# Fetching some chunks of a two-layer graph convolution row by row through SyncE

## The chip, the cores and the metric

The kernel runs on one core of one Trainium2 chip. The metric is the device time of one execution in microseconds. The kernel before the change takes 2024.17 us in the median of three runs (2023.47 to 2024.36).

## The reference

The input is a table of 6250 nodes with 512 features in float32 and a list of 100000 edges, sorted by their target node. Two Chebyshev graph convolutions follow each other, and the input is added at the end:

```
edge_index = jnp.stack([src, dst])
norm = -dinv[src] * dinv[dst]                  # dinv = 1/sqrt(out-degree), 0 for degree 0
def cheb_conv(x, W0, W1, b):
    tx1 = segment_sum(x[src] * norm[:, None], dst, num_segments=6250)
    return x @ W0 + tx1 @ W1 + b
h = relu(layernorm(x))
h = cheb_conv(h, W1_0, W1_1, b1)
h = layernorm(h) * gamma + beta
h = where(h >= 0, h, 0.01 * h)
out = x + cheb_conv(h, W2_0, W2_1, b2)
```

The part that matters here is `x[src]`: for every edge the row of its source node (512 float32, 2 KB) is fetched from a table in HBM, 100000 rows in each layer, and the rows of one target node are summed.

## The kernel before

The sorted edges are cut into 782 chunks of 128 edges. One chunk is one gather: `gather_to` lets GpSimd (POOL in the profile) issue one indirect DMA at L480, which reads 128 source indices from a column of `sidx` (for the last 270 chunks of layer 1 from `lidx`) and brings 128 rows, one into each partition, from the table of the layer, `tab[layer]`. A row of `tab[0]` is 528 floats wide: 512 features, then a scale of the row in column 512. The rows land in `places`, a tile of 63 places of 528 floats per partition, used as a ring: `slot(k)` names the place of the chunk with the running number k, and `zr(layer, t)` is the view of its 512 features. Of the 63 places the last 8 are lent to the second layer's weights (`w_late`, W2_1 and W2_0, loaded half way through layer 0), which leaves a ring of R = 55. The first 75 chunks of layer 0 are gathered straight from the input (L250) and put through layer norm on the chip; 27 chunks of layer 1 are gathered early, at L490 (`gather_ahead`).

Three chunks make a unit, and four units, so 12 chunks, a group; a layer has 66 groups. The loop over the groups g does, in this order: issue gathers as far as R chunks ahead of what has been summed; finish the node blocks that are complete (`finished`, `turn`); build the selection matrices `sel` on VectorE (`choose`; in layer 0 `scale`, L647, multiplies them by the rows' own scale out of column 512); sum the group on TensorE (`sums`, L660: one matmul of 128x32 by 128x512 for each chunk, into a PSUM tile `ps`); copy to `agg` (L673). A node block has 128 nodes, so there are 49 blocks a layer. For each block the sums are placed (`place`, L693), transposed (L803) and multiplied by the weights (`products`, L568), and `finish` writes the block: in layer 0 to `tab[1]` (L777) and `h_tab` (L782), in layer 1 to the output (L757).

The orders of TensorE, GpSimd and SyncE (SP) are written out by hand: what the loop emits first is issued first. SP's queue holds only ordinary DMAs: in layer 0 for each block the load of the block's own rows (`load_h`, L545), L777 and L782; in layer 1 L545, the load of the input's rows (L564) and L757. Several of them wait for TensorE or VectorE, and those behind them wait too.

Of the kernel before, what the change touches and what calls it, by code (L numbers as in the profile page):

```python
# [9 lines left out]
F32 = mybir.dt.float32  # L10
BF = mybir.dt.bfloat16
I32 = mybir.dt.int32
AF = mybir.ActivationFunctionType
OP = mybir.AluOpType
AX = mybir.AxisListType
# [3 lines left out]
SP = mybir.EngineType.SP  # L19

P = 128
# [4 lines left out]
Q = 32  # L26
NQ = P // Q
STEP = 3
DRIFT = 32
RE = 14  # L30
RAW = 76
PAD = 16
LATE = 3
AHEAD_OF = 27
JOIN = 12


def parts(r):
# [5 lines left out]
def gnn_kernel(  # L44
# [33 lines left out]
    nc = tc.nc  # L78
    N, D = x.shape
# [6 lines left out]
    NC = -(-E // P)  # L86
# [3 lines left out]
    NS = -(-NU // NQ)  # L90
    unit = [max(0, NU - NQ * (NS - g)) for g in range(NS + 1)]
    rows = [min(P, N - i * P) for i in range(NB)]
    LAST = 18
    W = D + PAD

    const = ctx.enter_context(tc.tile_pool(name="const", bufs=1))
# [6 lines left out]
    tab = [dram.tile([n, w], F32, name=f"tab{i}") for i, (n, w) in enumerate(((NB * P, W), (N + 1, D)))]  # L103
    zero_row = (NB - LATE) * P
# [3 lines left out]
    ident = const.tile([P, P], F32, name="ident")  # L108
    iota_r = const.tile([P, P], F32, name="iota_r")
    ones = const.tile([P, 1], F32, name="ones")  # L110
    eps = const.tile([P, 1], F32, name="eps")
# [16 lines left out]
    e_src = const.tile([P, AHEAD_OF, LATE], F32, name="e_src")  # L128
    w_sb = [const.tile([P, KD, D], F32, name=f"w{i}") for i in range(2)]
    sc = const.tile([P, 2, NB], F32, name="sc")  # L130
    pick = const.tile([P, P], BF, name="pick")
    src_lo = const.tile([P, P], BF, name="src_lo")
    src_hi = const.tile([P, RAW], F32, name="src_hi")
    p_id = const.tile([P, 1], F32, name="p_id")

# [288 lines left out]
    n_unseen = usual_path(tc, locals())  # L424
    stay.close()
    with tc.If(n_unseen > 0):
        general_path(tc, x, src, dst, bias1, bias2, gam, bet, w_sb, (W2_1, W2_0), dinv, ndinv, ident, iota_r,
                     eps, out)


def usual_path(tc, have):
    nc = tc.nc
    (x, out, tab, h_tab, ndinv, sidx, dlx, iota_r, w_sb, W2_1, W2_0, w_late, ident, eps, ones, first, nodes_ps, node_of, minus,
     unsorted, dinv, sdinv, bias1, bias2, gam, bet, unseen, unit, N, E, D, NB, NC, NU, NS, KD, rows, places, R,
     load_rest, sc, pick, src_lo, src_hi, eidx, e_src, zero_row, p_id, lent, X) = (
        have[n] for n in ("x out tab h_tab ndinv sidx dlx iota_r w_sb W2_1 W2_0 w_late ident eps ones first nodes_ps node_of "
                          "minus unsorted dinv sdinv bias1 bias2 gam bet unseen unit N E D NB NC NU NS KD rows places "
                          "R load_rest sc pick src_lo src_hi eidx e_src zero_row p_id lent X").split())
    AHEAD = 2
    SOON = range(3, 6)  # L440
    EARLY = {NB - 4: NS - 13, NB - 3: NS - 11, NB - 2: NS - 9, NB - 1: NS - 7}
# [9 lines left out]
    with ExitStack() as es:  # L451
# [11 lines left out]

        LATER = places.shape[1] - R

        def slot(k):
            return k - X if k < X + R + LATER else (k - X - LATER) % R

        def zr(layer, t):
            k = layer * NC + t  # L470
            return lent[k] if k < X else places[:, slot(k), :D]

        def gather_to(layer, summed_to):
            nonlocal gathered
            end = summed_to + R
            if layer == 0:
                end = max(end, min(end + LATER, X + LATER + 2 * R))
            for t in range(gathered, min(end, NC)):
                own_scale = layer == 0 and t >= RAW
                nc.gpsimd.indirect_dma_start(  # L480
                    out=places[:, slot(t), :] if own_scale else zr(layer, t), out_offset=None,
                    in_=x if layer == 0 and t < RAW else tab[layer],
                    in_offset=bass.IndirectOffsetOnAxis(
                        ap=lidx[:, t - SHIFTED : t - SHIFTED + 1] if layer and t >= SHIFTED else sidx[:, t : t + 1], axis=0))
            gathered = max(gathered, min(end, NC))
# [149 lines left out]
        def scale(sel, chunk, of=(0, NQ)):  # L635

            at = chunk[0][0]
            start = max(chunk[of[0]][0], RAW)
            end = chunk[min(of[1], len(chunk)) - 1][-1] + 1
            if end <= start:  # L640
                return
            each = sel.rearrange("p q s e -> p (q s) e")
            cut = sorted({start, end} | {t for t in range(start + 1, end) if slot(t) != slot(t - 1) + 1})
            for lo, hi in zip(cut, cut[1:]):
                v = each[:, lo - at : hi - at, :]
                k = slot(lo)
                last = nc.vector.tensor_tensor(  # L647
                    v, v, places[:, k : k + hi - lo, D : D + 1].to_broadcast([P, hi - lo, Q]), op=OP.mult)
            return last

        def sums(layer, g, sel, chunk, cnt=None, some=None, opens=True, closes=True):

            n = len(chunk)
            if opens:
                summed[0] = psum.tile([P, D], F32, name="ps")
            ps = summed[0]
            if some is None:
                some = [(s, q) for s in range(STEP) for q in range(n) if s < len(chunk[q])]
            for s, q in some:
                nc.tensor.matmul(ps[q * Q : (q + 1) * Q, :], sel[:, q, s, :], zr(layer, chunk[q][s]), start=(s == 0),  # L660
                                 stop=(s == len(chunk[q]) - 1 and (cnt is None or chunk[q][0] >= AHEAD_OF)))
            for b in range(LATE if cnt is not None else 0):
                r = rows[NB - LATE + b]
                for q in range(n):
                    if chunk[q][0] < AHEAD_OF:
                        nc.tensor.matmul(ps[q * Q : (q + 1) * Q, :], cnt[:r, b, q * Q : (q + 1) * Q],
                                         late[NB - LATE + b][:r], start=False, stop=(b == LATE - 1))
            if closes:
                wide = layer == 0 and g < SOON.stop + 2 and g % 2
                agg[g] = pool.tile([P, D], F32, name="pre" if wide else "agg", bufs=3)  # L670
                w = D // 2 if g == NS - 1 else D
                for lo in range(0, D, w):
                    nc.scalar.activation(agg[g][: n * Q, lo : lo + w], ps[: n * Q, lo : lo + w], AF.Copy)  # L673
# [212 lines left out]
        for layer in range(2):  # L886
# [5 lines left out]
            for g in range(NS - 1):  # L892
                gather_to(layer, STEP * unit[g])
                if layer == 0 and g == NS // 2:
                    for k, w in enumerate((W2_1, W2_0)):
                        nc.sync.dma_start(w_late[:, k], w.rearrange("(k p) d -> p k d", p=P))
                if layer == 0:
                    look_up("hT_ps")
                    find("hT_ps")
                    assert looked >= min(RAW, STEP * unit[g + 1])  # L900
                due = []

                def finished():
# [14 lines left out]
                if g == NS - 2 and layer == 0:  # L918
                    assert i >= NB - LATE and gathered == NC
                    gather_ahead()  # L920
                sel, chunk = chosen.pop(g) if g in chosen else choose(g)
                if layer == 0:
                    with ExitStack() as order:
                        for ins in behind.values():
                            order.enter_context(tc.issue_after(ins.ins))
                        scaled = scale(sel, chunk)
# [10 lines left out]
                if g < NS - 2:  # L937
                    sums(layer, g, sel, chunk, cnt)
                    if soon:
                        i, left = finished()  # L940
                else:
                    assert len(due) == 1 and due[0][0] == NB - 3 and all(len(c) == STEP for c in chunk)
                    if layer:
                        half = [[(s, q) for s in range(STEP) for q in range(at, at + NQ // 2)] for at in (0, NQ // 2)]
                        step = [half[0][:-2], half[0][-2:], half[1]]
                    else:
                        step = [[(s, q) for q in range(NQ)] for s in range(STEP)]
                    sums(layer, g, sel, chunk, None, step[0], True, False)
                    k, (hT, an) = due.pop()
                    aT = first_half(layer, k, hT, an, lambda: sums(layer, g, sel, chunk, None, step[1], False, False))  # L950
                    second(layer, k, aT)
                    sums(layer, g, sel, chunk, None, step[2], False, True)
                if layer == 0 and g == 12:
                    own_row[0] = pool.tile([P, D], F32, name="xt")
                    nc.vector.tensor_scalar_mul(own_row[0][:, : rows[END]], ident[:, : rows[END]], ndinv[:, END : END + 1])
# [70 lines left out]
    return n_unseen  # L1026


def general_path(tc, x, src, dst, bias1, bias2, gam, bet, w_sb, w_late, dinv, ndinv, ident, iota_r, eps,
                 out):  # L1030


# [31 lines left out]
    z_tab = [dram.tile([N, D], F32, name=f"z_tab{i}") for i in range(2)]  # L1064
    e_src = dram.tile([NC, P], I32, name="e_src")
    e_dst = dram.tile([NC, P], I32, name="e_dst")
    w_sb = list(w_sb)
    for k, w in enumerate(w_late):
        w_sb.append(const.tile([P, KD, D], F32, name=f"w_late{k}"))
# [284 lines left out]
```

## Time and profile before

| What | Value |
|---|---|
| median of the three runs | 2024.17 us |
| profiled execution | 2021.09 us, of which the span from the first to the last instruction is 2019.3 us |
| TensorE busy | 1669.7 us (83%), 6907 matmuls |
| GpSimd busy | 1488.9 us (74%), 1578 instructions |
| VectorE busy | 707.6 us (35%) |
| ScalarE busy | 414.3 us (21%) |
| moved by DMA | 528.41 MB, 262 GB/s |
| mean granted TensorE clock | 0.917 |

The busy time of GpSimd counts only the part of an indirect DMA in which its descriptors are made; the time between two of them counts as idle. The issue of a DMA by SP isn't counted as busy time of an engine at all; the views of a single line show it. The DMA share is the mean busy share of the core's 16 DMA engines.

### The profile page before, as it was taken

Reading aid. Unit: us, or ns where it says so; the run is one execution under the profiler, and the core shown is the slowest. Engines: PE = TensorE matmul, PEld = TensorE weight load, DVE = VectorE, ACT = ScalarE, POOL = GpSimd, SP = SyncE. Lnnn points to the kernel's source line nnn. Section 1 sums busy time; section 2 is a strip of 40 time slices with the busy share of each in tenths; the row PEclk is TensorE's granted clock in tenths of the full one; section 3 lists DMA queues with packets and bytes.
Section 4 is the critical chain, followed back from the end, with each engine's and each line's share of the span. In section 5 each row is a group of like instructions: output and inputs, shape, how many; then the busy total and the mean of one; then the engine's idle time right before and its main releaser. Section 6 shows DMA issues by size and latency. Waiting matters only on the chain.

```text
span 2019.3 us, 20097 instructions
## 1 busy us (share of the span) xinstructions
PE 1669.7 (83%) x6907; PEld 669.5 (33%) x6907; DVE 707.6 (35%) x1498; ACT 414.3 (21%) x752; POOL 1488.9 (74%) x1578
## 2 busy tenths in 40 slices
PE   5579998776887776888879888888888888888988
PEld 4444443222333222333323322323332223333333
DVE  7975554333354334343363111112221212222211
ACT  7895221111121111121111010011010001011100
POOL 6477777777777777777777777777777777777774
PEclk8789999888998888989999998889999989989999
DMA  9998888888988888888887787788787878788875
GB/s 329 396 374 269 267 269 263 249 258 245 303 265 253 251 260 241 267 266 260 245 261 241 245 257 247 247 252 255 240 255 246 254 244 257 241 263 251 272 235 171
DMA packets 190131, 528.41 MB, mean 262 GB/s; under 512 B 34652, under 2 KB 36426, under 8 KB 190020
## 3 DMA queue, kind: packets, MB, share of 16 engines
q0 software_dynamic: 125120, 415.88, 67.7%
q1 hardware_dynamic: 64860, 111.14, 15.2%
q8 instruction: 56, 0.92, 0.2%
q14 instruction: 55, 0.45, 0.1%
q10 hardware_dynamic: 40, 0.02, 0.0%
HBM read 475.25 MB, written 51.66 MB: 261 GB/s over the span
## 4 chain that ended last, share of the span: by engine, by line
PE 39%; DMA 31%; POOL 12%; issue 10%; DVE 5%; ACT 2%; POOLq 0%; DVEq 0%; SPq 0%; ACTq 0%
DMA places<-tab,sidx 24%; PE u_ps L568 16%; POOL places L480 12%; PE ps L660 12%; PE an_ps L693 7%; DMA places<-tab,lidx 5%; PE hT_ps L556 1%; PE hT_ps L803 1%; DVE hi L362 1%; DVE lo L362 1%; ACT places L539 1%; DMA dst_c<-in_dst_dram 1%; DMA tab<-places 1%; PE both_ps L379 1%; DVE sel L647 0%
## 5 line engine op out<-in xcount | busy, mean ns | idle before, releaser
L480 POOL DMA_INDIRECT places<-tab,sidx x1191 | 1130.5, 949 | 363.4 <-issue 256.2
L660 PE MATMUL ps<-places,sel 128*32 128x512 f32 x3104 | 517.1, 671 | 145.4 <-DMA places<-tab,sidx 81.9
L693 PE MATMUL an_ps<-agg,there 128*128 128x512 f32 (+1 forms) x554 | 270.0, 620 | 88.2 <-ACT agg L673 83.2
L480 POOL DMA_INDIRECT places<-tab,lidx x270 | 255.3, 946 | 82.3 <-issue 60.9
L660 PEld LDWEIGHTS ps<-places,sel 128*32 128x32 f32 x3104 | 103.1, 117 | 524.1 <-issue 190.0
L607 DVE TENSOR_TENSOR sel<-dlx,nodes_ps 128x384 f32<-128x384 f32 (+3 forms) x134 | 72.4, 541 | 415.1 <-PE ps L660 415.1
L568 PE MATMUL u_ps<-w,hT 128*128 128x512 f32 (+1 forms) x400 | 185.3, 607 | 20.6 <-ACT hT L558 20.1
L673 ACT ACTIVATE agg<-ps 128x512 f32<-128x512 f32 (+2 forms) x130 | 76.1, 587 | 570.1 <-PE ps L660 545.1
L568 PE MATMUL u_ps<-places,hT 128*128 128x512 f32 (+2 forms) x408 | 182.4, 591 | 2.9 <-ACT hT L558 2.9
L568 PE MATMUL u_ps<-w,aT 128*128 128x512 f32 x384 | 173.2, 594 | 2.7 <-DVE aT L805 2.7
L693 PEld LDWEIGHTS an_ps<-agg,there 128*128 128x128 f32 (+1 forms) x554 | 105.8, 199 | 209.6 <-issue 109.8
L568 PE MATMUL u_ps<-places,aT 128*128 128x512 f32 x384 | 173.5, 594 | 0.8 <-DVE aT L805 0.8
L647 DVE TENSOR_TENSOR sel<-sel,places 128x384 f32<-128x384 f32 (+11 forms) x71 | 34.4, 490 | 328.3 <-DMA places<-tab,sidx 323.2
L754 DVE TENSOR_TENSOR u_ps<-u_ps,bias 128x512 f32<-128x512 f32 x45 | 31.5, 700 | 281.8 <-PE u_ps L568 281.8
L558 ACT ACTIVATE hT<-hT_ps 128x512 f32<-128x512 f32 (+1 forms) x98 | 58.2, 594 | 278.1 <-PE hT_ps L556 277.6
L796 ACT ACTIVATE an<-an_ps,ndinv 128x512 f32<-128x512 f32 x96 | 65.8, 685 | 213.7 <-PE an_ps L693 213.5
L681 DVE TENSOR_SCALAR there<-iota_r,node_of 128x128 f32<-128x128 f32 (+1 forms) x286 | 85.8, 302 | 63.6 <-PE an_ps L693 61.3
L568 PEld LDWEIGHTS u_ps<-w,hT 128*128 128x128 f32 (+1 forms) x400 | 73.7, 195 | 96.5 <-issue 74.7
L766 ACT ACTIVATE sd<-mv,eps 128x1 f32<-128x1 f32 (+1 forms) x49 | 14.4, 294 | 433.5 <-DVE mv L764 433.5
L250 POOL DMA_INDIRECT places<-in_x_dram,sidx x63 | 60.0, 952 | 54.0 <-ACT junk L266 21.1
L568 PEld LDWEIGHTS u_ps<-places,hT 128*128 128x128 f32 (+1 forms) x408 | 74.4, 192 | 76.5 <-issue 71.5
L568 PEld LDWEIGHTS u_ps<-w,aT 128*128 128x128 f32 x384 | 70.7, 190 | 83.0 <-issue 77.8
(197 smaller groups left out, 1318.6 us busy)
## 6 DMA issues: line engine op xcount, KB each, us to landing
places<-tab,sidx POOLq DMA_INDIRECT x1191, 3.8
h_tab<-g SPq DMA_DIRECT2D x48, 256.0 KB
xt<-in_x_dram SPq DMA_DIRECT2D x48, 256.0 KB
out_dram<-t SPq DMA_DIRECT2D x48, 256.0 KB
tab<-t SPq DMA_DIRECT2D x46, 256.0 KB
tab<-places SPq DMA_DIRECT2D x22, 528.0 KB
h<-tab SPq DMA_DIRECT2D x45, 256.0 KB
h<-h_tab SPq DMA_DIRECT2D x45, 256.0 KB
```

What stands on the lines that cost most here:

```text
L250: nc.gpsimd.indirect_dma_start(out=lent[t] if t < X else places[:, t - X, :D], out_offset=None, in_=x, in_offset=bass.IndirectOffsetOnAxis ...
L362: nc.vector.tensor_tensor(t, s[:, g * 2 * GJ : (g + 1) * 2 * GJ].rearrange("p (j s) -> p j s", s=2)[:, :, None, :] .to_broadcast([EP, GJ, ...
L480: nc.gpsimd.indirect_dma_start(out=places[:, slot(t), :] if own_scale else zr(layer, t), out_offset=None, in_=x if layer == 0 and t < RAW ...
L558: nc.scalar.activation(hT[:, :, :r], ps[:, :, :r], AF.Copy)
L568: nc.tensor.matmul(u_ps[:r], hT[:, kc, :r], w[:, kc, :], start=(start and kc == 0), stop=(stop and kc == KD - 1))
L607: nc.vector.tensor_tensor(sel[:, q : q + k, :w, :], of, node[:, q : q + k, None, :].to_broadcast([P, k, w, Q]), op=OP.is_equal)
L647: last = nc.vector.tensor_tensor(v, v, places[:, k : k + hi - lo, D : D + 1].to_broadcast([P, hi - lo, Q]), op=OP.mult)
L660: nc.tensor.matmul(ps[q * Q : (q + 1) * Q, :], sel[:, q, s, :], zr(layer, chunk[q][s]), start=(s == 0), stop=(s == len(chunk[q]) - 1 and ( ...
L673: nc.scalar.activation(agg[g][: n * Q, lo : lo + w], ps[: n * Q, lo : lo + w], AF.Copy)
L681: behind[1] = nc.vector.tensor_scalar(t[:m, :r], iota_r[:m, :r], node_of[:m, g : g + 1], -(1.0 + i * P), op0=OP.subtract, op1=OP.is_equal)
L693: nc.tensor.matmul(placed[i][:r], t[:m, :r], agg[g][:m, :], start=(g == inside[i][0]), stop=(g == inside[i][-1]))
L796: nc.scalar.activation(an[:r], placed.pop(i)[:r], AF.Copy, scale=ndinv[:r, i : i + 1])
```

## The change

Fifteen chunks are no longer gathered by GpSimd: 7 of layer 0 (t = 206, 290, ..., 710) and 8 of layer 1 (t = 146, 230, ..., 734). Each is the last chunk of its group. SP fetches their 128 rows with 128 DMAs of one row each. For that SP loads the byte offsets of up to 9 rows from SBUF into registers (`starts`, made by `set_starts` from `src` with one DMA and a few VectorE operations for each layer) and issues one DMA per row with that register in its source address. A row is cut into 16 pieces: of 33 floats in layer 0 (the last of the 16 pieces ends with the scale; the pieces overlap by one float in the source, and the place is 16 x 33 floats), of 32 floats in layer 1. `fetch` is called twice in every group, once ahead of `finished` and once after the sums, and issues up to 9 rows each time, so 18 rows a group; it begins at group 7 of layer 0 and group 2 of layer 1. Two whole groups lie between the group that issues a chunk's last row and the group that sums the chunk.

In layer 0 the rows go to two of the places that W2_1 holds later, and the load of W2_1 moves from the middle of layer 0 to four groups before its end. In layer 1 they go to the tile of W1_0, which layer 1 no longer reads; `general_path`, which runs only for inputs that the usual path does not cover, therefore loads W1_1 and W1_0 again. `gather_to` skips the 15 chunks, `zr` gives the view of 16 pieces for them, the matmul's target is seen in the same shape, and `scale` multiplies such a chunk in an operation of its own.

```diff
+AT_ONCE = 9
+PIECES = (16, 16)
+ONE_BY_ONE = (7, 2)
+SECOND = 32
...
+    low_of = const.tile([P, 2, P], BF, name="low_of")
+    pick, src_lo = (low_of[:, k, :] for k in range(2))
+    starts = low_of.rearrange("p k e -> p (k e)").bitcast(I32)
...
+        one_by_one, to_fetch = {}, []
+        for layer, g in enumerate(ONE_BY_ONE):
+            for j in range(SECOND):
+                at = g + -(-P * (j + 1) // (2 * AT_ONCE)) + 2
+                if at > NS - 5:
+                    break
+                t = STEP * unit[at + 1] - 1
+                one_by_one[layer * NC + t] = (layer * SECOND + j, R + j % 2 if layer == 0 else j % 2)
...
+        def set_starts():
...
+                nc.sync.dma_start(starts[rows_of], bass.AP(tensor=src.tensor, offset=src.offset + some[0] * P,
+                                                           ap=[[step * P, n], [1, P]]))
+                nc.vector.tensor_copy(at, starts[rows_of])
+                if layer:
+                    nc.vector.tensor_single_scalar(up, at, float(zero_row), op=OP.is_ge)
+                    nc.vector.tensor_add(at, at, up)
+                nc.vector.tensor_scalar_mul(at, at, 4.0 * tab[layer].shape[1])
+                nc.vector.tensor_copy(starts[rows_of], at)
...
+        def spread(k):
+
+            at = one_by_one[k][1]
+            row = places[:, at, :] if k < NC else w_free[:, at * W : (at + 1) * W]
+            return row.rearrange("p (a b) -> p a b", a=PIECES[k // NC])
+
+        def fetch(layer):
+
+            some = to_fetch[:AT_ONCE]
+            del to_fetch[:AT_ONCE]
+            for t in sorted({t for t, _ in some}):
+                fetch_rows(layer, t, [e for of, e in some if of == t])
+
+        def fetch_rows(layer, t, es):
+
+            e, n = es[0], len(es)
+            at = one_by_one[layer * NC + t][0]
+            _, regs = nc.values_load_multi_w_load_instructions(
+                starts[at : at + 1, e : e + n], engines=(SP,), min_val=0, max_val=(tab[layer].shape[0] - 1) * tab[layer].shape[1] * 4,
+                skip_runtime_bounds_check_because="rows of the table")
+            flat = tab[layer].bitcast(U8).rearrange("n d -> (n d)")
+            w = PIECE[layer] + 1 - layer
+            flat = bass.AP(tensor=flat.tensor, offset=flat.offset,
+                           ap=[[1, flat.shape[0]], [PIECE[layer] * 4, PIECES[layer]], [1, w * 4]])
+            to = spread(layer * NC + t)[:, :, :w].bitcast(U8)
+            for j, start in enumerate(regs):
+                nc.sync.dma_start(to[e + j : e + j + 1], flat[bass.ds(start, 1)])
+
...
             for t in range(gathered, min(end, NC)):
+                if layer * NC + t in one_by_one:
+                    continue
...
-            cut = sorted({start, end} | {t for t in range(start + 1, end) if slot(t) != slot(t - 1) + 1})
+            cut = sorted({start, end} | {t for t in range(start + 1, end) if slot(t) != slot(t - 1) + 1
+                                         or t in one_by_one or t - 1 in one_by_one})
...
             for s, q in some:
-                nc.tensor.matmul(ps[q * Q : (q + 1) * Q, :], sel[:, q, s, :], zr(layer, chunk[q][s]), start=(s == 0),
+                rows_of = zr(layer, chunk[q][s])
+                to = ps[q * Q : (q + 1) * Q, :]
+                if len(rows_of.shape) > 2:
+                    to = to.rearrange("p (a b) -> p a b", a=PIECES[layer])
+                nc.tensor.matmul(to, sel[:, q, s, :], rows_of, start=(s == 0),
                                  stop=(s == len(chunk[q]) - 1 and (cnt is None or chunk[q][0] >= AHEAD_OF)))
...
                 if layer == 0 and g == NS // 2:
-                    for k, w in enumerate((W2_1, W2_0)):
-                        nc.sync.dma_start(w_late[:, k], w.rearrange("(k p) d -> p k d", p=P))
+                    nc.sync.dma_start(w_late[:, 1], W2_0.rearrange("(k p) d -> p k d", p=P))
+                if layer == 0 and g == NS - 4:
+                    nc.sync.dma_start(w_late[:, 0], W2_1.rearrange("(k p) d -> p k d", p=P))
...
+                if layer == 0 and g == ONE_BY_ONE[0] - 1:
+                    assert found == RAW
+                    set_starts()
+                if g == ONE_BY_ONE[layer]:
+                    assert not to_fetch and looked == RAW
+                    to_fetch.extend((t, e) for t in own_rows[layer] for e in range(P))
+                fetch(layer)
                 due = []
...
                     sums(layer, g, sel, chunk, None, step[2], False, True)
+                fetch(layer)
                 if layer == 0 and g == 12:
```

More of the change, by code (lines that the diff above doesn't have):

```diff
@@ L12 @@
 I32 = mybir.dt.int32
+U8 = mybir.dt.uint8
 AF = mybir.ActivationFunctionType
@@ L130, in gnn_kernel @@
     sc = const.tile([P, 2, NB], F32, name="sc")
-    pick = const.tile([P, P], BF, name="pick")
-    src_lo = const.tile([P, P], BF, name="src_lo")
+    low_of = const.tile([P, 2, P], BF, name="low_of")
+    pick, src_lo = (low_of[:, k, :] for k in range(2))
+    starts = low_of.rearrange("p k e -> p (k e)").bitcast(I32)
     src_hi = const.tile([P, RAW], F32, name="src_hi")
@@ L426, in gnn_kernel @@
     with tc.If(n_unseen > 0):
-        general_path(tc, x, src, dst, bias1, bias2, gam, bet, w_sb, (W2_1, W2_0), dinv, ndinv, ident, iota_r,
+        general_path(tc, x, src, dst, bias1, bias2, gam, bet, w_sb, (W1_1, W1_0), (W2_1, W2_0), dinv, ndinv, ident, iota_r,
                      eps, out)
@@ L434, in usual_path @@
      unsorted, dinv, sdinv, bias1, bias2, gam, bet, unseen, unit, N, E, D, NB, NC, NU, NS, KD, rows, places, R,
-     load_rest, sc, pick, src_lo, src_hi, eidx, e_src, zero_row, p_id, lent, X) = (
+     load_rest, sc, pick, src_lo, src_hi, eidx, e_src, zero_row, p_id, lent, X, starts, src, W) = (
         have[n] for n in ("x out tab h_tab ndinv sidx dlx iota_r w_sb W2_1 W2_0 w_late ident eps ones first nodes_ps node_of "
                           "minus unsorted dinv sdinv bias1 bias2 gam bet unseen unit N E D NB NC NU NS KD rows places "
-                          "R load_rest sc pick src_lo src_hi eidx e_src zero_row p_id lent X").split())
+                          "R load_rest sc pick src_lo src_hi eidx e_src zero_row p_id lent X starts src W").split())
     AHEAD = 2
@@ L464, in usual_path @@
         LATER = places.shape[1] - R
+        one_by_one, to_fetch = {}, []
[6 more added lines that the diff above has]
+                one_by_one[layer * NC + t] = (layer * SECOND + j, R + j % 2 if layer == 0 else j % 2)
+        own_rows = [sorted(k - layer * NC for k in one_by_one if k // NC == layer) for layer in range(2)]
@@ new lines, in set_starts @@
+        def set_starts():
+            for layer, some in enumerate(own_rows):
+                n, step = len(some), some[1] - some[0]
+                assert some == [some[0] + j * step for j in range(n)]
+                rows_of = slice(layer * SECOND, layer * SECOND + n)
+                at, up = (pool.tile([P, D], F32, name="xt")[rows_of, :P] for _ in range(2))
+                nc.sync.dma_start(starts[rows_of], bass.AP(tensor=src.tensor, offset=src.offset + some[0] * P,
[6 more added lines that the diff above has]
+                nc.vector.tensor_copy(starts[rows_of], at)
@@ new lines, in usual_path @@
+        PIECE = [D // k for k in PIECES]
+        w_free = w_sb[1].rearrange("p k d -> p (k d)")
+        def spread(k):
[7 more added lines that the diff above has]
+                fetch_rows(layer, t, [e for of, e in some if of == t])
@@ L466, in slot @@
         def slot(k):
+            if k in one_by_one:
+                assert k < NC
+                return one_by_one[k][1]
             return k - X if k < X + R + LATER else (k - X - LATER) % R
@@ L470, in zr @@
             k = layer * NC + t
+            if k in one_by_one:
+                return spread(k)[:, :, : PIECE[layer]]
             return lent[k] if k < X else places[:, slot(k), :D]
@@ L646, in scale @@
                 k = slot(lo)
+                of = W - W // PIECES[0] + PIECE[0] if lo in one_by_one else D
                 last = nc.vector.tensor_tensor(
-                    v, v, places[:, k : k + hi - lo, D : D + 1].to_broadcast([P, hi - lo, Q]), op=OP.mult)
+                    v, v, places[:, k : k + hi - lo, of : of + 1].to_broadcast([P, hi - lo, Q]), op=OP.mult)
             return last
@@ L921, in usual_path @@
                 sel, chunk = chosen.pop(g) if g in chosen else choose(g)
+                assert not any(t in own_rows[layer] and to_fetch and t >= to_fetch[0][0] for c in chunk for t in c)
                 if layer == 0:
@@ L1026, in usual_path, with general_path @@
     return n_unseen
-def general_path(tc, x, src, dst, bias1, bias2, gam, bet, w_sb, w_late, dinv, ndinv, ident, iota_r, eps,
+def general_path(tc, x, src, dst, bias1, bias2, gam, bet, w_sb, w_first, w_late, dinv, ndinv, ident, iota_r, eps,
                  out):
@@ L1066, in general_path @@
     e_dst = dram.tile([NC, P], I32, name="e_dst")
+    for t, w in zip(w_sb, w_first):
+        nc.sync.dma_start(t, w.rearrange("(k p) d -> p k d", p=P))
     w_sb = list(w_sb)
```

## The prediction

> **What bounds the kernel now.** I read the head of the page first: spans, busy times, and where the chain that ended last ran.
>
> ```profile
> span 2019.3 us, 20097 instructions
> PE 1669.7 (83%) x6907; PEld 669.5 (33%) x6907; DVE 707.6 (35%) x1498; ACT 414.3 (21%) x752; POOL 1488.9 (74%) x1578
> DMA  9998888888988888888887787788787878788875
> PE 39%; DMA 31%; POOL 12%; issue 10%; DVE 5%; ACT 2%; POOLq 0%; DVEq 0%; SPq 0%; ACTq 0%
> ```
>
> TensorE looks like the bound at 83%, and the DMA digits are high as well. The chain, however, alternates between PE, the landing of gathers and POOL, which is what a PE looks like that has caught up with its supply. So next the two groups of gathers (columns: line, engine, operation, count, busy us, mean ns, idle us just before) and what POOL waited for:
>
> ```profile
> L480 POOL DMA_INDIRECT places<-tab,sidx x1191 | 1130.5, 949 | 363.4 <-issue 256.2 <-DMA places<-tab,sidx 66.7 <-PE ps L660 15.2
> L480 POOL DMA_INDIRECT places<-tab,lidx x270 | 255.3, 946 | 82.3 <-issue 60.9 <-DMA places<-tab,lidx 13.7 <-PE ps L660 3.0
> ```
>
> ```profile
> POOL places L480 <- issue: 317.1, 1041, 0.3
> POOL places L480 <- DMA places<-tab,sidx: 66.7, 219, 0.3
> POOL places L480 <- PE ps L660: 18.3, 60, 0.3
> ```
>
> The last column of the waits is the longest one: 0.3 us for each releaser. POOL never really waits for a place to come free; the 0.3 us is what lies between any two gathers. The last row of gathers gives the cadence: (255.3 + 82.3) / 270 = 1.250 us each. So POOL's 74% is a queue that never stops. Twelve gathers make a group of 12 x 1.250 = 15.0 us. The stages say the same (columns: length, busy PE, PEld, DVE, ACT, POOL with counts, clock, DMA share, GB/s):
>
> ```profile
> 210.00:960.00 750.00, 611.25 (x2485) 241.36 (x2485) 302.06 (x683) 138.01 (x252) 567.84 (x599) 0.90 0.84 261
> 1085.00:1950.00 865.00, 751.00 (x2751) 272.84 (x2749) 179.71 (x387) 93.40 (x150) 654.42 (x692) 0.94 0.81 252
> ```
>
> 750 / 599 and 865 / 692 are 1.25 us for each gather in the middle of both layers, while PE idles 139 us in the first and 114 us in the second. Both layers run at the pace at which POOL makes descriptors. At the end:
>
> ```profile
> 1971.55 5.51 DMA places<-tab,lidx
> 1977.07 0.04 issue
> 1977.11 1.04 PE ps L660 x2
> ```
>
> The chain leaves the gathers for the last time at 1977 us; the 42 us after it are PE's own tail and don't change.
>
> **What is removed.** Fifteen gathers out of a queue that never stops: 15 x 1.250 = 18.75 us, 8.75 in layer 0 and 10.0 in layer 1. All lie in the two stages above, well ahead of the tail. PE must then do a group in 15.0 - 1.25 / 7.1 = 14.82 us, since one gather goes in every 128 / 18 = 7.1 groups. Its work is 611 / 750 x 15.0 = 12.2 us a group in layer 0 and 13.0 us in layer 1, so it follows. At the seam of the layers POOL's early gathers wait for rows that PE's last blocks write; those blocks hang on gathers that also come earlier, so the seam moves along.
>
> **What SP gets.** In the middle of the layers SP has three DMAs for each block:
>
> ```profile
> L545 SPq DMA_DIRECT2D h<-tab x45: 319/320/1032, 131.1 to 949.4; - x45
> L564 SPq DMA_DIRECT2D xt<-in_x_dram x50: 317/426/1565, 1051.8 to 1944.5; - x50
> L757 SPq DMA_DIRECT2D out_dram<-t x48: 332/338/424, 1090.7 to 2009.8; - x48
> L168 SPq DMA_DIRECT2D src_c<-in_src_dram x1: 247/247/247, 4.6 to 4.6; - x1
> ```
>
> ```profile
> 4.62 0.25 SPq L168 DMA_DIRECT2D src_c<-in_src_dram  x1
> 4.91 0.39 SPq L186 DMA_DIRECT2D places<-in_x_dram  x1
> ```
>
> ```profile
> L740 SPq TENSOR_LOAD <-unseen x1: 538/538/538, 2011.6 to 2011.6; - x1
> ```
>
> (Durations are minimum, median, maximum in ns.) The dearer layer, 1, spends 0.32 + 0.43 + 0.34 and three gaps, about 1.25 us, on a block, and 49 blocks in 66 groups make that 0.93 us a group; call it 1.0. So 13.8 us of each group are free for 18 rows: 0.77 us a row. A row costs three things.
>
> - The issue: between 0.247 us (L168, one row) and 0.426 us (L564). I take 0.320, the median for a table in HBM that the kernel itself wrote (L545), which is what a row comes from.
> - The gap to the next: L168 ends at 4.87 and the next starts at 4.91, so 0.04; 0.05 with rounding.
> - The register: one load of one value took 0.538 us. The change asks for 9 values in one call. If that is one trip it is 0.06 us a row, if nine, 0.538. No row decides; I take the middle, 0.30.
>
> Sum 0.32 + 0.05 + 0.30 = 0.67 us a row, 12.1 us a group, 13.1 with SP's own DMAs: it fits into 14.82 with 1.7 to spare. From the ends: 0.25 + 0.04 + 0.06 = 0.35 and 0.43 + 0.05 + 0.54 = 1.02 us a row, 7.3 and 19.4 us a group. So fitting is likely, not certain. The Trainium skill (Runtime: NRT & Kernel Launch, section Instruction fetch mechanics) puts a register load at about 200 ns for each register even in bulk; by that the sum would be 0.57 us a row and 11.3 us a group, and no run so far shows a load of several.
>
> What queues behind these rows is SP's own work: the load of a block two blocks ahead, the stores, in layer 1 the input's rows, all issued some 5 us later than now. They have a block, some 20 us, to land, so I cost this at nothing while SP keeps up. Two whole groups, 30 us, lie between a chunk's last issue and its sum; a gather lands in about 4 us:
>
> ```profile
> DMA to landing us min/median/max: 3.5/3.8/5.9
> ```
>
> **What the DMA engines get.** One gather takes (window 1200 to 1400, 160 gathers) 0.695 x 200 / 160 = 0.87 us of all 16 engines. A row by SP is 16 pieces, and 16 completions if it behaves as the DMAs there do: 29 DMAs of 128 rows show 4176 packets, 144 each. That is 4096 small packets a chunk.
>
> ```profile
> DMA packets 16991, 49.70 MB, mean 248 GB/s; under 512 B 3024, under 2 KB 3024, under 8 KB 16982
> q0 software_dynamic: 12806, 41.98, 69.5%
> q1 hardware_dynamic: 4176, 7.60, 10.5%
> places<-tab,sidx POOLq DMA_INDIRECT x160, 3.8
> h<-h_tab SPq DMA_DIRECT2D x10, 256.0 KB
> out_dram<-t SPq DMA_DIRECT2D x10, 256.0 KB
> xt<-in_x_dram SPq DMA_DIRECT2D x9, 256.0 KB
> ```
>
> ```profile
> DMA packets 144, 0.07 MB, mean 131 GB/s; under 512 B 16, under 2 KB 144, under 8 KB 144
> q1 hardware_dynamic: 144, 0.07, 45.8%
> ```
>
> The last fence is a window of 0.5 us (1.7 to 2.2) that holds one load of 512-byte pieces alone: 0.458 x 16 x 0.5 / 144 = 25 ns a packet. So a chunk would take 4096 x 25 / 16 = 6.5 us of the engines, in place of 0.87, once in 7.1 groups (105 us): 5.3 points of share, 0.84 to 0.89 in layer 0 and 0.81 to 0.86 in layer 1. That is room enough, and I take it. The price is bounded below by nothing (the gather's 0.87 us then comes back, 0.8 points) and above by the 80 ns that a packet of that mix took, most of 2 KB (0.105 x 16 x 200 / 4176).
>
> **The small edits.** The matmul of one chunk and the scaling of a group in layer 0 have these rows:
>
> ```profile
> L660 PE MATMUL ps<-places,sel 128*32 128x512 f32 x3104 | 517.1, 671 | 145.4 <-DMA places<-tab,sidx 81.9 <-DMA places<-tab,lidx 35.2 <-DVE sel L647 22.4
> L647 DVE TENSOR_TENSOR sel<-sel,places 128x384 f32<-128x384 f32 (+11 forms) x71 | 34.4, 490 | 328.3 <-DMA places<-tab,sidx 323.2 <-issue 5.1
> ```
>
> Fifteen matmuls read 16 pieces of a row with a float between them; if each took twice the 671 ns of L660, 10 us, they would sit in the 253 us that PE idles. Seven more scalings at 490 ns (L647) and some ten operations for the offsets lie in VectorE's idle time, 448 of the 750 us. W2_1's load, 1 MB, comes four groups, 60 us, ahead of its use; at the stages' 250 GB/s it takes 4 us if alone. All at nothing; without the cover a few us.
>
> **Sum.** Against the profiled execution, 2021.09 - 18.75 = 2002.3 us. The median of the runs is 3.1 us above it, so 2024.17 - 18.75 = 2005.4 us, 0.9% faster.
>
> **Rivals.**
> - *SP becomes the pace.* Mechanism: nine values are nine trips, and a row costs 0.538 + 0.32 + 0.05 = 0.91 us. A group then takes SP 18 x 0.91 + 1.0 = 17.4 us against 15.0. The 1920 rows are 106.7 groups; less the 30 us of cushion in each layer that is 106.7 x 2.4 - 60 = 196 us: 2220 us. It decides from 0.81 us a row, where 106.7 x (18 x 0.81 + 1.0 - 15.0) is the cushion. For it: one value already takes 0.538 us, and register arithmetic ahead of a DMA is in no row. Against it: the rows are asked for in one call, and mid-values leave 1.7 us. An overrun by a little, 0.84 us a row, gives 60 us more than now, 2084 us.
> - *The DMA engines fill up.* At 80 ns a packet a chunk takes 20.5 us, 19 points more: 1.03 in layer 0, 1.00 in layer 1. Layer 0's 49.8 groups stretch by 3% (about 22 us) in place of losing 8.75; layer 1 keeps its 10: 2036 us. Against it: the 25 ns row, and the stage from 100 to 200 us (the row below). The Trainium skill (DMA: Bandwidth & Descriptors, sections Rules for kernel authors and Specifications) speaks for it: it wants transfers coalesced, since under 64 KB one pays mostly overhead, and pieces of at least 512 B. The trace agrees that small pieces are dear by the byte (25 ns for 512 B, 80 ns in a mix mostly of 2 KB), not that they fill the engines.
> - *The saving is spent again.* Every fetched chunk makes PE wait about as long as a gather, 1.25 us, by late rows or by the waits on 128 completions: 2024 us. Against it: two groups of cushion.
>
> ```profile
> 100.00:200.00 100.00, 83.73 (x467) 45.59 (x468) 63.80 (x150) 74.97 (x111) 74.49 (x79) 0.92 0.96 324
> ```
>
> At a share of 0.96, POOL still made 79 gathers in 100 us, so a share of 0.89 is no reason for it to slow down.
>
> **Numbers.** The forecast has 64%, SP as the pace 24%, full DMA engines 6%, the saving spent again 6%. A measurement of this kernel can tell about 0.2% from no change. So faster 0.64, same 0.06, slower 0.30. The forecast's own range is 2002 (a little more gained, from the runs' spread and a shorter landing) to 2015 (half the gain lost to small waits). To hold 8 in 10 the range takes in the 2024 and 2036 of the smaller rivals and the milder third of the overruns, up to 0.84 us a row: 2002 to 2090 us.
>
> **What would show it.** Right: the two L480 groups at 1179 and 267, 15 fewer in all, still 1.25 us apart; groups of 14.8 us; SP's TENSOR_LOAD for 9 values below 3 us and its DMAs for a row about 0.32 us; a DMA share of 0.86 to 0.89 in the middle of the layers. Wrong: PE (L660) waiting for DMAs of SP for tens of us, POOL waiting for PE at L480 by more than 0.3 us, or a cadence of gathers above 1.25 us.

## The result: 10% slower

The changed kernel takes 2232.32 us in the median (2230.51 to 2242.66, 4 runs), the kernel before 2023.93 us in the same runs: a ratio of 1.104, 95% interval 1.1006 to 1.1075. That is 208 us more, where 18.75 us less were forecast. In five of the seven sets of runs under Experiments (e1 to e4, e7 to e10, e14 to e18) the kernel before itself took 2449 to 2471 us and every variant beside it more than that, with stops that the waits put down to "remote", so their whole times decide nothing and only the lengths of single instructions are used from them.

The head of the page after, and the two groups of gathers:

```profile
span 2228.7 us, 24299 instructions
PE 1622.0 (73%) x6907; PEld 689.4 (31%) x6907; DVE 711.0 (32%) x1513; ACT 416.2 (19%) x752; POOL 1473.9 (66%) x1563
SPq 40%; PE 35%; DMA 11%; DVE 6%; issue 6%; ACT 1%; POOL 0%; DVEq 0%; ACTq 0%; POOLq 0%
SPq L527 27%; PE u_ps L638 17%; SPq L518 11%; PE ps L736 8%; PE an_ps L769 6%; DMA h<-tab 3%; DMA h<-h_tab 3%; PE hT_ps L626 2%; DMA tab<-places 1%; DVE hi L368 1%; DVE lo L368 1%; PE hT_ps L879 1%; DMA w<-in_L_gnn_W_dram 1%; SPq L634 1%; DMA h_tab<-g 1%
...
L550 POOL DMA_INDIRECT places<-tab,sidx x1179 | 1119.0, 949 | 477.6 <-issue 272.7
L550 POOL DMA_INDIRECT places<-tab,lidx x267 | 252.6, 946 | 135.7 <-issue 63.4
```

POOL has 12% of the chain before and 0% now; SP has gone from 0% to 40%, with two lines: L527, the DMA of a row, and L518, the load of offsets. The gathers are 1179 and 267, 15 fewer, and one still takes 0.949 us, so the saving was made. But POOL now idles. The middle of both layers, by busy time (the second window begins later than before, since layer 1 does):

```profile
210.00:960.00 750.00, 513.33 (x2058) 208.01 (x2057) 255.50 (x582) 116.42 (x208) 500.93 (x528) 0.83 0.77 229
1160.00:1950.00 790.00, 566.67 (x2355) 225.10 (x2352) 157.26 (x345) 77.17 (x127) 576.05 (x608) 0.85 0.79 239
```

POOL makes 528 gathers in 750 us, one in 1.42 us, and the DMA share has fallen from 0.84 and 0.81 to 0.77 and 0.79 in place of rising: the DMA engines are less busy than before, which speaks against them as what is late (e6 below settles it). Who waits for whom, and what SP waits for (first row before, second after):

```profile
PE hT_ps L626 <- DMA h<-tab: 228.1, 19, 20.3
DVE t L831 <- DMA xt<-in_x_dram: 256.7, 23, 21.3
PE hT_ps L626 <- DMA h<-h_tab: 224.5, 22, 20.0
POOL places L550 <- PE ps L736: 195.3, 77, 14.2
PE ps L736 <- DMA places<-tab,sidx: 9.7, 4, 3.8
```

```profile
SPq L545 <- PE hT_ps L556: 545.4, 65, 20.9
```

```profile
SPq L615 <- PE hT_ps L626: 17.8, 4, 15.7
```

PE does not wait for the rows that are fetched one by one. It waits, up to 20 us at a time, for `h`, the block's own rows, and VectorE for `xt`: plain loads that stand in SP's queue behind the rows. SP used to reach the load of `h` early and wait 545 us there for PE; now it comes too late for it, and waits 18 us there in all. That makes SP the likely pace; its own time says how.

### The profile page after: what moved, and what is told of

Its sections match the earlier page's. It is cut to its first block, busy times and chain, and to the rows that moved or that the text cites. A ratio compares the mean times of both kernels' runs of the same rounds, so it can differ in the third digit from the quotient of the medians.

```text
span 2228.7 us, 24299 instructions
## 1 busy us (share of the span) xinstructions
PE 1622.0 (73%) x6907; PEld 689.4 (31%) x6907; DVE 711.0 (32%) x1513; ACT 416.2 (19%) x752; POOL 1473.9 (66%) x1563
## 4 chain that ended last, share of the span: by engine, by line
SPq 40%; PE 35%; DMA 11%; DVE 6%; issue 6%; ACT 1%; POOL 0%; DVEq 0%; ACTq 0%; POOLq 0%
SPq L527 27%; PE u_ps L638 17%; SPq L518 11%; PE ps L736 8%; PE an_ps L769 6%; DMA h<-tab 3%; DMA h<-h_tab 3%; PE hT_ps L626 2%; DMA tab<-places 1%; DVE hi L368 1%; DVE lo L368 1%; PE hT_ps L879 1%; DMA w<-in_L_gnn_W_dram 1%; SPq L634 1%; DMA h_tab<-g 1%
## 5 line engine op out<-in xcount | busy, mean ns | idle before, releaser
L626 PE MATMUL hT_ps<-ident,h 128*128 128x128 f32 x360 | 71.4, 333 | 452.6 <-DMA h<-tab 228.1
L736 PE MATMUL ps<-places,sel 128*32 128x512 f32 x3088 | 390.2, 606 | 13.5 <-DMA places<-tab,sidx 9.7
L769 PE MATMUL an_ps<-agg,there 128*128 128x512 f32 (+1 forms) x554 | 256.4, 597 | 0.0
L626 PEld LDWEIGHTS hT_ps<-ident,h 128*128 128x128 f32 x360 | 48.9, 168 | 518.0 <-issue 500.9
L638 PE MATMUL u_ps<-w,aT 128*128 128x512 f32 x384 | 206.3, 688 | 1.9 <-DVE aT L881 1.9
L638 PE MATMUL u_ps<-places,aT 128*128 128x512 f32 x384 | 206.0, 686 | 0.8 <-DVE aT L881 0.8
L836 DVE TENSOR_TENSOR u_ps<-u_ps,bias 128x512 f32<-128x512 f32 x45 | 31.5, 700 | 370.8 <-PE u_ps L638 360.8
L830 DVE TENSOR_TENSOR u_ps<-u_ps,bias 128x512 f32<-128x512 f32 x45 | 31.5, 700 | 279.0 <-PE u_ps L638 279.0
L638 PEld LDWEIGHTS u_ps<-w,aT 128*128 128x128 f32 x384 | 84.6, 228 | 102.8 <-issue 99.5
L831 DVE TENSOR_TENSOR t<-u_ps,xt 128x512 f32<-128x512 f32 x45 | 30.9, 687 | 266.2 <-DMA xt<-in_x_dram 256.7
L638 PEld LDWEIGHTS u_ps<-places,aT 128*128 128x128 f32 x384 | 84.1, 227 | 100.8 <-issue 98.8
```

Source lines behind the costliest of these rows:

```text
L626: nc.tensor.transpose(ps[:, kc, :r], h[:r, kc * P : (kc + 1) * P], ident[:r, :r])
L638: nc.tensor.matmul(u_ps[:r], hT[:, kc, :r], w[:, kc, :], start=(start and kc == 0), stop=(stop and kc == KD - 1))
L736: nc.tensor.matmul(to, sel[:, q, s, :], rows_of, start=(s == 0), stop=(s == len(chunk[q]) - 1 and (cnt is None or chunk[q][0] >= AHEAD_OF)))
L769: nc.tensor.matmul(placed[i][:r], t[:m, :r], agg[g][:m, :], start=(g == inside[i][0]), stop=(g == inside[i][-1]))
```

## What a row costs SP

The lines of the row and of the load in the changed kernel (minimum, median, maximum in ns; first and last start), and a piece of the chain that runs on SP alone (start, length):

```profile
L527 SPq MOVE w<-tab x1024: 29/29/29, 1178.1 to 2147.7; - x171
L527 SPq DMA_DIRECT2D w<-tab x1024: 506/537/1742, 1178.2 to 2147.7; - x171
L527 SPq DMA_DIRECT2D places<-tab x896: 506/537/1530, 194.1 to 1066.4; - x180
```

```profile
L518 SPq TENSOR_LOAD <-low_of x227: 279/1876/3739, 192.9 to 2142.3; - x114
```

```profile
1298.69 2.47 SPq L518
...
1302.54 0.54 SPq L527
1303.17 0.54 SPq L527
...
1306.90 0.47 SPq L518
...
1308.67 0.94 SPq L518
...
1314.14 0.53 SPq L833
...
1314.71 2.17 SPq L518
```

1024 rows in layer 1 take from 1178 to 2148 us: 17.0 us for each 18. In layer 0 it is 872 us for 896 rows, 17.5 us for 18. A row starts 0.632 us after the one before it at the median (0.63 from 1302.54 to 1303.17): 0.537 for the DMA, 0.029 for the move of its register, the rest gaps. So 18 rows are 11.4 us; two loads at the median are 3.8 us; 1.8 us remain for SP's own DMAs, for waits and for whatever is longer than its median. That is 17.0 us where POOL needs 14.82, and SP itself waits for only 15 of the 872 us and 26 of the 970.

## Experiments

Theory A: SP's own time is the pace. Rival B: the rows' small packets, or the waits for their completions. Each time stands beside that of the kernel before in the same set of runs.

**Fewer rows a group.** `AT_ONCE = 9` becomes 8 (e1) or 7 (e2, and again e5).

> 8 rows at once instead of 9, so 16 a group and 6 + 7 = 13 chunks. Theory A (SP's own time is the pace: in the changed kernel a row costs it 0.64 us of issue, register move and gaps, a load about 1.7 us for each burst, its own DMAs 1.4 us a group, 17.0 us in all against 15.0 for twelve gathers): 16 x 0.64 + 1.4 = 11.6 us and two loads; with loads as long as before 15.1 us a group, about 2030 us, with loads that get shorter because 8 values now start on a 16-byte boundary 13.5 us, and then POOL is the pace again: 2024 - 13 x 1.25 = 2008 us. Rival B (the small packets of the rows on the DMA engines, or the waits for the rows' completions, are the pace): the rows per group fall by a ninth and so does the loss: about 2024 + 227 x 8/9 - 16 = 2210 us.

> 7 rows at once, 14 a group, 5 + 6 = 11 chunks. Theory A: 14 x 0.64 + 3.4 + 1.4 = 13.8 us of SP a group, below POOL's 14.86, so the saving comes through whole: 2024 - 11 x 1.25 = 2010 us. Rival B: 2024 + 227 x 7/9 - 14 = 2187 us.

> The kernel with 7 rows at once (14 a group, 11 chunks) again, since the kernel before itself took 2465 us in the first set instead of 2024. Theory A (SP's own time is the pace) where the kernel before takes 2024 us: 14 x 0.64 + two loads of at most 1.7 us + 1.4 = 13.8 us of SP a group, below POOL's 14.86, so 2024 - 11 x 1.25 = 2010 us. Rival B (the rows' small packets or their completions): 2187 us.

e1 took 2695.4 and e2 2616.45 us where the kernel before took 2465.36: no answer. e5: 2008.58 us against 2022.23, ratio 0.9932 (0.991 to 0.9953). With 14 rows a group the loss is gone, not smaller by two ninths, and the saving of 11 gathers (13.75 us) is there whole. Rival B would have 2187. From e1 comes one row: with 8 at once every load begins on a multiple of eight values, and it takes 0.531 us instead of 1.876:

```profile
L518 SPq TENSOR_LOAD <-low_of x208: 3/531/2342, 256.4 to 2586.1; - x104
```

The same kernel ran three times more: 2632.05 us (e8), 2679.97 (e15) and 2682.32 (e17), where the kernel before took 2449.41, 2470.92 and 2463.36. Its whole time stays open.

> 8 rows at once (16 a group, 13 chunks) on a chip where the kernel before takes 2024 us: all loads begin on a multiple of 8 and take 0.53 us. Theory A: 16 x 0.632 + 1.1 + 1.4 = 12.6 us of SP a group: POOL stays the pace, 2024 - 13 x 1.25 = 2008 us.

**The same rows without loads and registers.** Addresses are constants of the program; the rows fetched are then not those of the edges.

```diff
-            _, regs = nc.values_load_multi_w_load_instructions(starts[...], engines=(SP,), ...)
+            regs = [((t * P + e + j) * 7 % (N - P)) * tab[layer].shape[1] * 4 for j in range(n)]
...
-                nc.sync.dma_start(to[e + j : e + j + 1], flat[bass.ds(start, 1)])
+                nc.sync.dma_start(to[e + j : e + j + 1], flat[start : start + 1])
```

> 18 rows a group as in the change, but each row's address is a constant of the program: no load of offsets, no register (the rows that are fetched are not the ones that the edges name; everything else is as in the change). The same number of DMAs, pieces and completions. Theory A: the loads (0.19 us a row) and the register moves (0.06) go, a row costs at most 0.58 us and SP at most 18 x 0.58 + 1.4 = 11.8 us a group: about 2005 us; if the issue falls from 0.54 towards the 0.32 of the plain DMAs, the register is what made it dear. Rival B: no change, 2232 us.

> Again 18 rows a group with constant addresses, no load and no register (other rows than the edges name are fetched). In the first set a row was issued every 0.632 us with a constant just as with a register, so the register itself costs nothing beside the issue and only the loads fall away. Theory A: 18 x 0.632 + 1.4 = 12.8 us of SP a group against POOL's 14.82: 2005 us. Rival B: 2232 us.

e3 took 2580.04 us where the kernel before took 2465.36. e6: 2004.04 us (2 runs) against 2022.23, ratio 0.9906 (0.988 to 0.9933). That is 18.2 us less, the forecast's saving to within a microsecond, with all 15 chunks, all 30720 pieces and all completions. This rules out rival B. A row's DMA with a constant, in layer 1 and in layer 0:

```profile
L525 SPq DMA_DIRECT2D w<-tab x1024: 481/587/1990, 1043.7 to 1920.3; - x171
L525 SPq DMA_DIRECT2D places<-tab x896: 481/587/1809, 187.1 to 927.0; - x180
```

0.587 us plus a gap is the same 0.632 us as with a register: addressing by a register is free, loading it is not. PE still waits 92 us for `h` in layer 0 of e6, and 123 us in e5, so SP runs close to the pace even where nothing is lost.

**The load alone.** Each load begins on a multiple of 4 values and takes whole fours.

```diff
+            e0 = e - e % 4
-                starts[at : at + 1, e : e + n], ...
+                starts[at : at + 1, e0 : e0 + -(-(e + n - e0) // 4) * 4], ...
+            regs = regs[e - e0 : e - e0 + n]
```

> The change with one edit: each load of offsets begins on a multiple of 4 values and takes whole fours, so 12 registers at most, of which the burst uses its 9. In the changed kernel a load of 9 values took 0.757 us when it began on a multiple of 4 and 1.87 to 2.75 us when it didn't. Theory A with the alignment as the term that tips it: two loads of 0.8 us, 18 x 0.632 + 1.6 + 1.4 = 14.4 us a group, just under POOL's 14.82, so 15 chunks' saving: 2005 us. If alignment is not what makes the loads long (12 values simply take longer than 9): 2 x 2.9 us and 18.6 us a group, 2024 + 106.7 x 3.6 - 60 = 2350 us.

> 18 rows a group, 16 pieces, each load of offsets from a multiple of 4 values on (0.745 us for 12 in the set before, against 1.87 to 2.75). Where the kernel before takes 2024 us, theory A gives 18 x 0.632 + 2 x 0.8 + 1.4 = 14.4 us of SP a group, just under POOL's 14.82: 2005 us. If the loads are not the term that tips it: 2150 us or more.

e11: 2061.63 us against 2021.13, ratio 1.0191 (1.017 to 1.0211); e7 took 2762.21 us where the kernel before took 2449.41.

```profile
L519 SPq TENSOR_LOAD <-low_of x227: 293/757/2581, 195.5 to 1976.5; - x114
```

```profile
L529 SPq DMA_DIRECT2D w<-tab x1024: 506/537/1333, 1097.5 to 1981.0; - x171
L529 SPq DMA_DIRECT2D places<-tab x896: 506/537/1874, 196.7 to 983.0; - x180
```

The load falls from 1.876 to 0.757 us in the median, and the loss from 208 us to 40. The trace of the changed kernel has the same split: of its loads of 9 values the 50 that begin on a multiple of four take 0.757 us at the median, the other 149 take 1.90 (1.86 to 3.74).

But 2005 was expected. My 14.4 us was worked out from medians, and the tail is missing in it. It lies in layer 0: its 896 rows take 786.3 us, against 739.9 in e6, where the saving came through, while the 1024 rows of layer 1 take 883.5 against 876.6. Layer 0's 106 loads average 1.15 us, layer 1's 121 average 0.80. Why a load takes longer in layer 0 is not shown.

**The issue alone.** `PIECES = (16, 16)` becomes (4, 4) in e4 and e9, (1, 1) in e10 and e12.

> 4 pieces a row instead of 16, all else as in the change. If the issue time of a row hangs on its number of pieces, as it might since 16 pieces are 16 descriptors, it falls from 0.54 to perhaps 0.40 us and theory A gives 18 x 0.70 + 1.4 = 14.0 us a group, 2005 us; if it doesn't, theory A gives 2232 us again. Rival B has a quarter of the packets and gives about 2024 + 227 / 4 - 19 = 2060 us either way.

> 4 pieces a row, 18 rows a group, loads as in the change, on a chip where the kernel before takes 2024 us. The first set showed an issue of 0.577 us with 4 pieces against 0.537 with 16, so fewer pieces do not make the issue cheaper. Theory A: 0.04 us a row more than the change, 0.7 us a group: 2232 + 106.7 x 0.7 = 2307 us. Rival B (the number of small packets): about 2060 us.

> One piece of 2 KB a row, 18 rows a group, loads as in the change. If the issue falls to the 0.247 us that the kernel before shows for a transfer of one piece, theory A gives 18 x 0.36 + 3.5 + 1.4 = 11.4 us a group: 2005 us; if the issue stays at 0.55 us, 2232 to 2300 us. Rival B: a sixteenth of the packets, 2024 + 227 / 16 - 19 = 2020 us.

> 18 rows a group, loads as in the change, one piece of 2 KB a row, whose issue took 0.228 us in the set before. Theory A: 18 x (0.228 + 0.095) + 3.5 + 1.4 = 10.7 us of SP a group: 2005 us, unless the one DMA engine that then carries all these rows (128 packets of 90 ns, 12 us a chunk, 12 points of its share) becomes late, which would show as PE waiting for gathers.

e4 (3023.58 us, the kernel before 2465.36), e9 (2955.43) and e10 (2584.39, both beside 2449.41) show only the issue, 0.577 us for 4 pieces and 0.228 for one. e12: 2003.73 us against 2021.13, ratio 0.9921 (0.99 to 0.9942).

```profile
L527 SPq DMA_DIRECT2D w<-tab x1024: 227/228/305, 1044.8 to 1911.3; - x171
L518 SPq TENSOR_LOAD <-low_of x227: 467/2126/4085, 195.0 to 1907.1; - x114
```

```profile
PE ps L736 <- DMA places<-tab,sidx: 77.2, 46, 4.0
PE hT_ps L626 <- DMA h<-tab: 54.5, 11, 8.5
SPq L833 <- DVE t L831: 188.8, 25, 12.7
```

Loads as long as ever, rows at less than half: 1024 rows take 866.5 us, much as in e6. SP is no longer the pace: it waits for VectorE again, 189 us at the store L833. PE waits for gathers first of all, as in the kernel before, though 54.5 us of waits for `h` are left. So taking away either term alone, the loads (e6) or most of the issue (e12), is enough; the issue is the larger, 18 x 0.31 = 5.6 us a group against 3.8. This version is 0.8% faster than the kernel before, and 10% faster than the changed kernel.

**More chunks with cheap rows.** One piece and `AT_ONCE = 16`: 27 chunks (e13).

> One piece a row and 16 rows at once, so 32 a group, one chunk every 4 groups, 13 + 14 = 27 chunks; 16 values a load, always from a multiple of 16 on. Theory A: 32 x 0.323 + 2 x 1.0 + 1.4 = 13.7 us of SP a group, POOL 15.0 - 1.25 / 4 = 14.69, PE 12.2 to 13.0: 2024 - 27 x 1.25 = 1990 us. Against it: one DMA engine carries 12 us more in every 59 us, 20 points on a share of 81 to 84; if that engine fills up, the gathers land late and it takes some 2000 to 2030 us.

2156.1 us against 2021.13, ratio 1.0662 (1.0644 to 1.0681): a miss. Below are the load and the row, then waits, then the landing of the gathers between 1200 and 1400 us:

```profile
L518 SPq TENSOR_LOAD <-low_of x216: 1157/1255/2849, 195.1 to 2057.0; - x108
L527 SPq DMA_DIRECT2D w<-tab x1792: 227/228/474, 1133.3 to 2063.8; - x200
```

```profile
PE hT_ps L626 <- DMA h<-h_tab: 207.3, 21, 18.7
SPq L527 <- DMA w<-tab: 31.4, 88, 1.3
SPq L527 <- DMA places<-tab: 27.0, 68, 1.4
DMA to landing us min/median/max: 3.7/4.0/6.6
```

SP is late again: 1792 rows in 930.5 us are 16.6 us for 32, where 13.7 were expected and POOL needs 14.69; PE again waits for `h`. But the reason is only in part the same. Of the 2.9 us too many, 0.9 are the loads (1.255 us at the median instead of 1.0, and a tail). Another 1.3 are waits at L527 for DMAs of SP's own that have not landed, 88 times for rows in layer 1 and 68 times in layer 0; the landing of these rows has 14% of the chain (8.6% and 5.8%). That is the second part of rival B, which e6 excludes for 16 pieces and nine rows in a row; here it counts.

In the traces each row's DMA waits on the semaphore of the DMA that SP issued eight before it. In one piece eight issues take 8 x 0.324 = 2.6 us, and a row lands (the last increment of its semaphore) 2.6 to 2.7 us after its issue at the median, so sixteen in a row run into the wait. In the changed kernel eight issues take 5.1 us and a row lands in 3.0, which leaves nothing to wait for. The rows land as fast in e13 as in e12 and the gathers in 4.0 us, before in 3.8, so nothing shows that what carries the rows has filled up.

**In between: 13 rows at once**, one piece, loads on multiples of four, 21 chunks (e14, e16 and e18, the same kernel).

> One piece a row, 13 rows at once, 21 chunks, aligned loads, once more. Where the kernel before takes about 2022 us: 13.1 us of SP a group, POOL 14.75: 1996 us if SP's time per row is the whole limit; 2005 us or more if the one DMA engine that carries all the rows, or another stage, is one too.

2818.28, 2819.44 and 2761.68 us, the kernel before 2456.55 to 2470.92: no answer. Whether 21 chunks pay stays open.

## Why the prediction was wrong

- *What bounds the kernel, and what is removed:* right. e6 gets the 18.75 us to within its error (2022.23 - 2004.04 = 18.2), e12 17.4, e5 13.7 of 13.75.
- *The issue of a row, 0.32 us:* this step failed. I took the plain load of 128 rows (L545) as the nearest; a single row in 16 pieces takes 0.537, and with move and gaps 0.63 instead of 0.37. Even the upper end, 0.426, was too low. The row that I had for a single transfer, 0.247, is near what one piece costs (0.228), and e12 with it comes to within 2 us of the forecast.
- *The register, 0.30 us a row:* too high, and on the safe side; 1.876 / 9 = 0.21 at the median. The page of the Trainium skill that I set beside it (Runtime: NRT & Kernel Launch, Instruction fetch mechanics: about 200 ns a register even in bulk; it speaks of registers loaded from HBM, and these come from SBUF) was the better price. The trace agrees where a load begins off a multiple of four values; e11 shows 0.76 us for 12 registers, 0.063 each, where it begins on one.
- *The sum:* 13.1 us a group were forecast and 17.0 measured in layer 1: issue, move and gaps 11.4 in place of 6.7, loads 3.8 in place of 5.4, SP's own DMAs with waits and long issues 1.8 in place of 1.0. So a row costs 0.63 + 0.21 = 0.84 us. My limit of 0.81 was passed by 0.03, and that decides the sign, not the size: by my own formula 0.84 costs 60 us. The rest of the 208 is in the groups, which took 17.5 and 17.0 us instead of 16.1 (119 us), and in a cushion of 30 us instead of 60.
- *"SP becomes the pace"*, at 24% and 2220 us, is what happened, at 2232. Its place was right and its mechanism half: not nine trips of 0.538 us (4.8 us a load), but a dear issue and loads of 1.9 us. That its time came so near is in part luck: its row is dearer, SP's other work cheaper and its cushion twice as large as measured.
- *SP's own loads at nothing while it keeps up:* the reservation was right. But I gave an overrun two groups of cushion, 30 us a layer, since I looked for the late one at the rows' chunks. It is the plain load behind them, with a block's slack. The sum of the group times, 49.8 x 2.5 + 56.9 x 2.0 = 238 us, less the 208 measured leaves 30 us of cushion in both layers together.
- *The DMA engines:* my fill-up rival is excluded by e6, and the small packets were priced too dear, at 5.3 points of share. In the middle of the layers (210 to 960 and 1085 to 1900 us) e6 with 16 pieces a row and e12 with one both have 0.86 and 0.82, the kernel before 0.84 and 0.81. The Trainium skill's warning against small transfers (DMA: Bandwidth & Descriptors, Rules for kernel authors: under 64 KB one pays mostly overhead) holds here for the queue that issues them: a chunk row by row takes SP 128 x 0.63 = 81 us, and a plain load of 128 rows 0.32. The engines that carry them show nothing of it.

## What to carry to other kernels

Before work goes to an idle queue, price it by the queue's own time for each instruction, of the same shape as the new one, and add that up against the pace of the loop; a queue with 0% of the chain can be full after eighteen small transfers in 15 us. When it overruns, look at what stands behind the new work in the same queue: here the first thing late was a plain load that nobody had touched. Of the remedies, one piece a row (e12) kept all 15 chunks and fewer rows (e5) kept 11; loads that begin on a multiple of four (e11) were not enough by themselves, and 4 pieces were no cheaper to issue than 16. With a cheaper issue more of them are in flight, and the wait for earlier ones to land becomes a price of its own (e13).

## What the hardware showed that was not expected

- A DMA of one row from SP took 0.228 us in one piece (e12), 0.577 in 4 (e4) and 0.537 in 16 (the changed kernel), all medians. Why 4 are dearer than 16 is not known.
- A constant address was no cheaper than one from a register: a row every 0.63 us either way.
- A load of offsets into registers took 0.53 us for 8 values from a multiple of eight on (e1), 0.76 for 9 or 12 from a multiple of four on (the changed kernel, e11), 1.255 for 16 from a multiple of sixteen on (e13), and 1.90 for 9 that begin anywhere else.
- A row fetched by SP landed 2.6 to 2.7 us after its issue in one piece and 3.0 in 16 (medians; e12, e13 and the changed kernel).
